# Attention block on one core: the next image's statistics and normalisation placed one by one on ScalarE, and the last residual loads given tiles and a queue of their own

## The chip, the cores and the metric

The kernel runs on one core of one Trainium2 chip. A core has five engines that run beside each other and meet at semaphores: TensorE (matmul, PE in the profile; its weight loads are PEld), VectorE (DVE), ScalarE (ACT), GpSimd (POOL) and SyncE (SP). SP, ACT and POOL each also have a queue on which DMA transfers are issued. The metric is device microseconds of one execution; the kernel before takes 3188.57 us, the median of 5 runs (3187.05 to 3190.02).

## The reference, cut to what matters

The input x has 16 images of 512 channels and 32 x 32 = 1024 pixels, in float32. Each image is normalised in 8 groups of channels, goes through attention with 4 heads of 128 channels over its 1024 pixels, is projected, and is added to itself.

```
mu, var = mean and variance of each group of channels
xn  = (xg - mu) * rsqrt(var + EPS) * gamma + beta
q, k, v = split(einsum('oc,bchw->bohw', qkv_w, xn) + qkv_b, 3)
attn = softmax(einsum('bhnd,bhmd->bhnm', q, k) * dh ** -0.5)
out = einsum('bhnm,bhmd->bhnd', attn, v)
out = einsum('oc,bchw->bohw', proj_w, out) + proj_b
return x + out
```

The last line is the residual: x has to be read a second time where the projection's results are ready.

## The kernel before, in words

The whole work is one stream of steps (`steps` = 16 images x 4 heads x 8 key blocks). In step s the main loop does two halves. In each half it gives TensorE the scores of one key block against 512 queries (`scores`, matmul L789, into one of two PSUM banks s) and the weighted sum of the step before (`weighted_sum`, L885, into po). ScalarE turns the scores into exponentials p (L795) and VectorE adds p to the running denominator tot (L803). Behind the two matmuls of a half stands half of the step's *units*: pieces of other work that `plan_head` (L1027) writes by hand into a list `plan[j]` for each of the head's 8 key blocks j. The first half of the list runs in the first half of the step, the rest in the second.

Head 0 of an image carries the q and k projection of its own heads 2 and 3, head 1 the output projection of the image *before* (`proj_groups`, names pp), head 2 the q and k projection of the *next* image's heads 0 and 1, and head 3 the next image's v. So what the next image needs must be ready by the end of head 1: its x is loaded there (`load_x`, in `plan[0]`), its statistics are taken, and it is normalised in place. In image 0 head 1 has no output projection, and in the last image no next image.

The statistics are `stats_chunk` for each of 4 chunks of 128 channels (two passes over 128 x 1024 on ScalarE, L243 and L246, with small scalings L244, L245 and L249 between them) and then `stats_group` once, which calls `Norm.group`: mean (L50, VectorE), a small matmul pm (L52, TensorE), d, mu and d2 (L55 to L61) and vv (L59) on VectorE, a small matmul pv (L63), ve (L65, VectorE), rstd as a power on GpSimd (L67), and sc, t and sh on VectorE (L69, L76, L78). `normalise` is one ScalarE instruction over 128 x 512 (L85, x<-x,sh,sc); there are 8 for an image, 4 chunks by 2 halves. `x_sums` (L280) then forms sums of the normalised x on VectorE. Before, `plan_head` puts two `stats_chunk` at the end of each of `plan[2]` and `plan[3]`, `stats_group` at the end of `plan[4]`, and four `normalise` at the end of each of `plan[5]` and `plan[6]`.

The projections are a matrix product in two levels of seven products instead of eight. The outer level has four groups g (`OUTER`); in each group, the inner level (`strassen`, L445) runs the products p1, p2, p6, p5, p7, p4, p3 in two PSUM banks x and y (matmuls L564). Between them ScalarE copies bank x out (p1, u2, u3: L458, shown as pp_u, pp_p) and bank y is added to such a copy by VectorE (L584) into a result tile r. The next product into a bank waits until the copy has been made. The inner results are c11, c22, c21 and c12; `combine` (L631) joins the groups' results, and `finish` (L766) adds bias and residual: for each 128 x 512 piece of an image's output one VectorE instruction y = r + bias + y (L769), one y = y + r (L772), and a DMA to out (L773).

The residual y is loaded by `prepare` (L753), two pieces for each of c11, c22, c21 and c12: into a tile of `ypool`, which has 4 buffers, by GpSimd's queue (L756). A fifth load therefore waits until an earlier piece has been stored. The c12 pieces, loaded for the last group, are the last two of the eight. `tpool` has one buffer for each tag; its tags ot40 and ot41 hold sums of the heads' outputs (t4) that TensorE reads in the output projection. SP's queue carries the weights of the groups (L371).

Which engine runs what is fixed in the code; the order on each engine is made by a scheduler that follows the program's order, except that `tc.high_priority(URGENT)` lets exponentials and the copies between products go ahead of other work. `tc.issue_after(ins)` keeps the instructions within it from being placed ahead of `ins`. [...]

```
for half in range(NH2):
    scores(s, half)
    weighted_sum(s - 1, half)
    n = (len(units) + 1) // 2
    run(units[half * n : (half + 1) * n])
```

Of the kernel before, what the change touches and what calls it, by code (L numbers as in the profile page):

```python
# [10 lines left out]
F32 = mybir.dt.float32  # L11
# [5 lines left out]
P = 128  # L17
# [4 lines left out]
HALF = 512  # L22
# [133 lines left out]
KC = 2  # L156
# [6 lines left out]
def fast_path(ctx, tc, x, sources, out, consts, flag, dims):  # L163
# [6 lines left out]
    nc = tc.nc  # L170
    B, C, N, NCC, NH2, NB, GC, SCALE = dims
# [9 lines left out]
    tpool = ctx.enter_context(tc.tile_pool(name="t", bufs=1))  # L181
# [7 lines left out]
    ypool = ctx.enter_context(tc.tile_pool(name="y", bufs=4))  # L189
# [44 lines left out]
    def stats_chunk(b, c):  # L234
        if c == 0:
            mvs[b] = gn.tile([P, NCC, 2], F32, tag="mv", name=f"mv_{b}")
        if b == 0:
            norm.chunk(mvs[b], xs[b, c], c)
            return

        junk = lpool.tile([P, N], F32, tag="tt", name=f"junk_{b}_{c}")
        sums = gn.tile([P, 3], F32, tag="st", name=f"sums_{b}_{c}")
        nc.scalar.activation(junk, xs[b, c], AF.Identity, accum_out=sums[:, 0:1])  # L243
        nc.scalar.mul(mvs[b][:, c, 0:1], sums[:, 0:1], 1.0 / N)  # L244
        nc.scalar.mul(sums[:, 1:2], sums[:, 0:1], -1.0 / N)  # L245
        nc.scalar.activation(  # L246
            junk, xs[b, c], AF.Square, bias=sums[:, 1:2], accum_out=sums[:, 2:3]
        )
        nc.scalar.mul(mvs[b][:, c, 1:2], sums[:, 2:3], 1.0 / N)  # L249

    def stats_group(b):
        mu, sc = norm.group(mvs.pop(b))
        scaled[b] = sc, norm.shift(mu, sc)

    def normalise(b, c, half):
        t = xs[b, c][:, ts(half, HALF)]
        sc, sh = scaled[b]

        return norm.apply(t, t, sc, sh, c, b > 0 or c % 2 == 1)
# [16 lines left out]
    def sums_of_b(b, rows=(1, 2, 3), chunks=range(KC)):  # L276

        def sub(o, i, j):
            for k in chunks:
                nc.vector.tensor_sub(b[o][k], b[i][k], b[j][k])  # L280

        if 1 in rows:
            sub("t1", "b12", "b11")
        if 2 in rows:
            sub("t2", "b22", "t1")
        if 3 in rows:
            sub("t3", "t2", "b11")
            sub("t4", "b21", "t2")

    def x_sums(b, rows=(1, 2, 3)):  # L290
        if 1 in rows:
            xb[b] = halves([xs[b, c] for c in range(NCC)], "x")
        sums_of_b(xb[b], rows)

    def o_blocks(b):
        ob[b] = halves([os_[b, h] for h in range(HEADS)], "o")
# [35 lines left out]
    def stage_blocks(site):  # L332

        raw = raw_blocks(site)
        st = stage[site] = {}
        names = ("a11", "a12", "a21", "a22", "s1", "s2")
        if site in ("proj", "v"):
            for n in names[:4]:
                st[n] = ypool.tile([P, HALF], F32, tag="y", name=f"st_{n}")
            for i, n in enumerate(names[4:]):  # L340
                st[n] = tpool.tile([P, HALF], F32, tag=f"ot2{i}", name=f"st_{n}")
        else:
            for i in range(3):
                t = opool.tile([P, N], F32, tag="o", name=f"st_{site}_{i}")
                for h in range(2):
                    st[names[2 * i + h]] = t[:, ts(h, HALF)]
        for n in names[:4]:
            load_block(st[n].rearrange("p (s d) -> p s d", d=P), raw[n])
# [397 lines left out]
    def proj_groups(b):  # L746

        ys = {}

        def place(which, r):  # L750
            return 2 * (int(which[1]) - 1) + r, int(which[2]) - 1

        def prepare(which, r):  # L753
            o, half = place(which, r)
            t = ys[which, r] = ypool.tile([P, HALF], F32, tag="y", name=f"y_{b}_{o}_{half}")
            dma = nc.gpsimd.dma_start(t, x[b, ts(o, P), ts(half, HALF)])  # L756

            tc.add_manual_dep(
                dma.ins, last_eviction[b].ins.name,
                mybir.DependencyInfo(  # L760
                    mybir.DependencyClass.Sync, mybir.DependencyReason.DATA
                ),
                reason="residual",
            )

        def finish(which, r, a, c):  # L766
            o, half = place(which, r)
            t = ys.pop((which, r))
            nc.vector.scalar_tensor_tensor(  # L769
                t, a, projb_sb[:, o : o + 1], t, ALU.add, ALU.add  # L770
            )
            nc.vector.tensor_add(t, t, c)  # L772
            nc.gpsimd.dma_start(out[b, ts(o, P), ts(half, HALF)], t)  # L773

        return two_levels(f"pp_{b}", "proj", b, lambda: ob[b], finish, prepare=prepare)
# [3 lines left out]
    inverse, rows_of, added, exps = {}, {}, {}, {}  # L779
    steps = B * HEADS * NB  # L780

    def where(s):
        bh, j = divmod(s, NB)
        return (*divmod(bh, HEADS), j)
# [112 lines left out]
    def spread(plan, units, first, last):  # L897

        for i, u in enumerate(units):
            plan[first + i * (last - first) // len(units)].append(u)  # L900
# [15 lines left out]
    def kept_group(site, g):  # L916
        if g == 0:
            stage_sums(site)
        group_weights(site, g, True)

    def staggered(lists):


        starts = (0, 4, 8, 16)[: len(lists)] if len(lists) != 3 else (0, 4, 10)
        at = [(a + i, g, u) for g, (a, us) in enumerate(zip(starts, lists))
              for i, u in enumerate(us)]
        return [u for _, _, u in sorted(at, key=lambda t: t[:2])]
# [33 lines left out]
    def last_projection(b):  # L961
# [12 lines left out]
        def add(row, r, half, a, done):  # L974
            o = 2 * row + r
            t = y[o][:, ts(half, HALF)]
            nc.vector.tensor_add(t, t, a)
            if done:
                (nc.sync, nc.scalar)[r].dma_start(out[b, ts(o, P), ts(half, HALF)], t)
# [43 lines left out]
        for r in range(2):  # L1023
            mm(y_[r], r, 3, False)
            add(0, r, 1, y_[r], True)

    def plan_head(b, h):  # L1027

        plan = [[] for _ in range(NB)]
        if h == 0:  # L1030
            spread(plan, staggered(next_qk.pop()), 0, NB)
            if b > 0:
                plan[6].append(lambda: o_blocks(b - 1))
                plan[6].append(lambda: sums_of_b(ob[b - 1]))
            else:
                plan[5].append(lambda: stage_blocks("v"))
        elif h == 1:
            if b > 0:
                spread(plan, staggered(proj_groups(b - 1)), 0, NB)
            if b + 1 == B:  # L1040
                plan[0].append(lambda: last_loads("x"))
            else:
                plan[0].append(lambda: load_x(b + 1))
                spread(plan, [lambda c=c: stats_chunk(b + 1, c) for c in range(NCC)], 2, 4)
                plan[4].append(lambda: stats_group(b + 1))
                for r in range(2):
                    plan[5 + r] += [
                        lambda c=c, half=half: normalise(b + 1, c, half)
                        for c in range(KC * r, KC * r + KC) for half in range(NH2)
                    ]  # L1050
                plan[6].append(lambda: x_sums(b + 1, (1,)))
            if b == 0:
                for g in range(len(OUTER)):
                    plan[g // 2].append(lambda g=g: kept_group("v", g))
                    plan[NB // 2 + g].append(lambda g=g: kept_group("proj", g))
                plan[2].append(lambda: stage_blocks("proj"))
                spread(plan, [lambda o=o: bias_of_v(o) for o in range(NCC)], 3, 5)
        elif b + 1 == B:
            if h == 2:
                plan[0].append(lambda: last_loads("w"))  # L1060
                plan[2].append(last_bias)
            else:
                os_[b, h] = opool.tile([P, N], F32, tag="o", name=f"o_{b}_{h}")
                plan[3].append(lambda: o_blocks(b))
                plan[3].append(lambda: sums_of_b(ob[b], (1,)))
                plan[5].append(lambda: sums_of_b(ob[b], (2, 3), (0,)))
        elif h == 2:
            spread(plan, staggered(qk_groups(b + 1, 0)), 0, NB)

            plan[0].insert(2, lambda: x_sums(b + 1, (2,)))  # L1070
            plan[1].append(lambda: x_sums(b + 1, (3,)))
        else:

            spread(plan, staggered(next_v.pop()), 0, NB - 1)

            plan[NB - 2].append(lambda: ahead[f"qk_{b + 1}_1"]())
        return plan
# [33 lines left out]
    plan = []  # L1111
    for s in range(steps + 1):
        units = []
        if s < steps:
            b, h, j = where(s)
            if j == 0:
                plan = plan_head(b, h)
# [157 lines left out]
```

## Time and profile before

| what | value |
|---|---|
| median of 5 runs | 3188.57 us (3187.05 to 3190.02) |
| profiled execution, its own time | 3187.58 us |
| its span in the profile | 3185.8 us |
| TensorE busy | 3156.0 us (99%), granted clock 1.00 |
| VectorE busy | 2632.2 us (83%) |
| ScalarE busy | 1443.6 us (45%) |
| GpSimd busy | 527.7 us (17%) |
| one image in the middle | 196.4 us |
| L85, normalisation, each (124 in all, 4 of them image 0's own) | 810 ns |
| L756, residual loads | 120, of 256 KB each |

An image in the middle repeats every 196.4 us, so head 1 of image 6 lies at about 1276 to 1325 us. In the lines below, a timeline shows start (us), duration (us), engine, line of the code, operation, out<-in with shapes, a count of equal instructions that were merged into one row, and in brackets how long the engine stood still before it and who ended that. A float32 matmul shows as two records; each runs on into the next, so TensorE's pace is read from start to start and not from the durations.

### The profile page before, as it was taken

What the parts mean: (1) busy time and instruction counts of PE and PEld (TensorE: products, weight loads), DVE (VectorE), ACT (ScalarE), POOL (GpSimd) and SP (SyncE); (2) the same over time, 40 slices, a digit from 0 to 9 for tenths busy, and PEclk for the clock granted to TensorE, in tenths of its full rate; (3) what the DMA queues carried; (4) which work ended last, traced back from release to release, by engine and by line L of the source; (5) the groups of instructions that cost most, each with busy time, mean ns of one, the idle gap of its engine ahead of it and who ended that gap; (6) DMA issues with size and microseconds to landing.
All of it is one profiled execution on the core that took longest, in us unless ns stands there. A gap on an engine that the chain in (4) does not pass through costs nothing.

```text
span 3185.8 us, 34047 instructions
## 1 busy us (share of the span) xinstructions
PE 3156.0 (99%) x10474; PEld 2182.5 (69%) x10474; DVE 2632.2 (83%) x4625; ACT 1443.6 (45%) x2709; POOL 527.7 (17%) x922
## 2 busy tenths in 40 slices
PE   8999999999999999999999999999999999999999
PEld 6566676676766766667666767667666676766764
DVE  8878878788897888878888787987879878788784
ACT  2535435354353543535435354453534545344342
POOL 0011221111211112211122111222112221122200
PEclk9999999999999999999999999999999999999999
DMA  5654554545545455454554545555355553555531
GB/s 169 216 184 153 188 174 151 172 147 196 169 159 167 153 184 174 164 167 143 194 170 161 175 137 189 172 171 177 132 178 169 175 179 133 184 160 183 182 126 41
DMA packets 209387, 526.92 MB, mean 165 GB/s; under 512 B 32816, under 2 KB 65840, under 8 KB 209200
## 3 DMA queue, kind: packets, MB, share of 16 engines
q1 hardware_dynamic: 128992, 276.88, 27.6%
q0 software_dynamic: 66240, 212.39, 19.6%
q10 hardware_dynamic: 13968, 35.41, 3.5%
q8 instruction: 86, 1.41, 0.2%
q14 instruction: 101, 0.83, 0.1%
HBM read 389.56 MB, written 135.00 MB: 165 GB/s over the span
## 4 chain that ended last, share of the span: by engine, by line
PE 85%; issue 5%; DVE 4%; DMA 2%; ACT 2%; POOL 1%; SPq 0%; ACTq 0%; POOLq 0%; DVEq 0%
PE po L885 24%; PE s L789 23%; PE qk_x L564 12%; PE qk_y L564 9%; PE v_x L564 6%; PE v_y L564 4%; PE pp_x L564 4%; PE pp_y L564 3%; ACT x L85 1%; DVE pp_r L631 1%; DMA y<-in_x 1%; POOL rstd L67 1%; DMA out_y<-y 1%; DVE pp_r L584 1%; DVE tot L803 1%
## 5 line engine op out<-in xcount | busy, mean ns | idle before, releaser
L885 PE MATMUL po<-p,v 128*128 128x512 f32 x2048 | 1048.9, 594 | 0.0
L789 PE MATMUL s<-qk,qk 128*128 128x512 f32 x2048 | 1047.1, 593 | 1.3 <-ACT p L795 1.3
L795 ACT ACTIVATE p<-s 128x512 f32<-128x512 f32 x1024 | 610.8, 597 | 944.6 <-PE s L789 904.2
L885 PEld LDWEIGHTS po<-p,v 128*128 128x128 f32 x2048 | 602.9, 303 | 316.8 <-issue 212.1
L803 DVE TENSOR_TENSOR tot<-tot,p 128x1024 f32<-128x1024 f32 x385 | 470.1, 1221 | 162.4 <-ACT p L795 162.4
L789 PEld LDWEIGHTS s<-qk,qk 128*128 128x128 f32 x2048 | 387.6, 190 | 89.2 <-issue 28.0
L564 PEld LDWEIGHTS qk_x<-qk_t,w 128*128 128x128 f32 x1344 | 250.6, 190 | 171.3 <-issue 76.4
L564 PE MATMUL qk_x<-qk_t,w 128*128 128x256 f32 x1344 | 357.2, 382 | 1.1 <-ACT qk_u L458 1.1
L458 ACT COPY qk_u<-qk_x 128x512 f32<-128x512 f32 (+1 forms) x256 | 136.4, 533 | 232.2 <-PE qk_x L564 224.5
L728 POOL DMA_DIRECT2D vd<-vu x120 | 66.6, 557 | 909.5 <-DVE vu L720 905.9
L584 DVE TENSOR_TENSOR qk_r<-qk_y,qk_u 128x512 f32<-128x512 f32 (+1 forms) x256 | 158.7, 620 | 36.3 <-ACT qk_u L458 22.2
L564 PE MATMUL pp_x<-pp_t,w_proj 128*128 128x256 f32 x630 | 169.4, 385 | 6.1 <-ACT pp_u L458 5.8
L773 POOL DMA_DIRECT2D out_y<-y x120 | 66.2, 552 | 615.2 <-DVE y L772 585.2
L733 POOL DMA_DIRECT2D v<-vd x240 | 140.5, 592 | 162.7 <-DMA vd<-vu 64.9
L584 DVE TENSOR_TENSOR v_r<-v_y,v_u 128x512 f32<-128x512 f32 (+1 forms) x120 | 76.1, 634 | 110.6 <-ACT v_u L458 80.3
L564 PE MATMUL v_x<-v_t,w_v 128*128 128x256 f32 x630 | 166.6, 381 | 0.0
L538 POOL DMA_DIRECT2D kept_t<-qk_t x240 | 129.2, 540 | 224.1 <-DVE qk_t L534 158.2
L564 PEld LDWEIGHTS pp_x<-pp_t,w_proj 128*128 128x128 f32 x630 | 115.4, 190 | 73.3 <-issue 22.2
L564 PEld LDWEIGHTS v_x<-v_t,w_v 128*128 128x128 f32 x630 | 118.4, 190 | 55.3 <-issue 19.1
L564 PE MATMUL qk_y<-x,w 128*128 128x256 f32 x512 | 141.7, 379 | 0.0
L663 DVE SCALAR_TENSOR_TENSOR qk<-qk_r,qkb_sb,qk_r 128x512 f32<-128x512 f32 x192 | 137.9, 746 | 1.6
L458 ACT COPY v_u<-v_x 128x512 f32<-128x512 f32 (+1 forms) x124 | 66.3, 535 | 160.2 <-PE v_x L564 130.3
(204 smaller groups left out, 4489.1 us busy)
## 6 DMA issues: line engine op xcount, KB each, us to landing
kept_t<-qk_t POOLq DMA_DIRECT2D x180, 256.0 KB, 3.1
w<-kept SPq DMA_DIRECT2D x90, 512.0 KB, 4.1
v_t<-kept_t SPq DMA_DIRECT2D x180, 256.0 KB, 2.9
w<-kept SPq DMA_DIRECT2D x90, 384.0 KB, 3.4
rinv<-row ACTq DMA_DIRECT2D x63, 512.0 KB, 4.8
x<-in_x POOLq DMA_DIRECT2D x60, 512.0 KB, 5.0
vd<-vu POOLq DMA_DIRECT2D x120, 256.0 KB, 3.0
v<-vd POOLq DMA_DIRECT2D x240, 128.0 KB, 4.0
```

Of the source, the lines that this page charges most:

```text
L458: nc.scalar.copy(t[n][:, :width], t["x"][:, :width])
L538: nc.gpsimd.dma_start(t, to)
L564: nc.tensor.matmul(acc[:, ts(i, Q)], have["w"][t][:, i, slot, :], inner(i, bn), start=(first and i == 0), stop=True, skip_group_check=True,)
L584: nc.vector.tensor_add(dst, view(a), view(c))
L663: nc.vector.scalar_tensor_tensor(st[b, h][:, ts(half, HALF)], a, qkb_sb[:, i : i + 1], c, ALU.add, ALU.add)
L728: nc.gpsimd.dma_start(rows[which][ts(h, P), :], u)
L733: nc.gpsimd.dma_start(vs[b, pair][ts(q, BLK), half].rearrange("m h (k i) j -> m (h k) (i j)", k=n), rows[which].rearrange("(k m) (q e) -> ...
L773: nc.gpsimd.dma_start(out[b, ts(o, P), ts(half, HALF)], t)
L789: nc.tensor.matmul(sc, ks[b, h][:, ts(j, P)], qs[b, h][:, ts(half, HALF)], start=True, stop=True)
L795: exps[s] = nc.scalar.activation(ps[s][:, ts(half, HALF)], sc, AF.Exp, scale=SCALE)
L803: added[b, h, j] = nc.vector.tensor_add(tot[b, h][:, i], tot[b, h][:, i], ps[s][:, i])
L885: nc.tensor.matmul(po[b, h][:, i], v_block(b, h, j), ps[s][:, i], start=(j == 0), stop=(j == NB - 1),)
```

## The change

In `prepare`, the c12 pieces take tiles of `tpool` with tags ot40 and ot41 in place of `ypool`'s, and are loaded by SP's queue in place of GpSimd's. In `plan_head`, the units of the next image's statistics and normalisation are laid one by one into successive half key blocks by a new helper `single`: the four `stats_chunk` from the second half of key block 1 to the first half of block 3, `stats_group` at the end of block 3, seven `normalise` from the second half of block 4 to the second half of block 7, and the eighth at the end of block 7. Another new helper, `behind_exps`, keeps each `stats_chunk` and `normalise` behind the latest exponential issued so far. No computation is added or left out.

```
         def prepare(which, r):
             o, half = place(which, r)
-            t = ys[which, r] = ypool.tile([P, HALF], F32, tag="y", name=f"y_{b}_{o}_{half}")
-            dma = nc.gpsimd.dma_start(t, x[b, ts(o, P), ts(half, HALF)])
+            own = which == "c12"
+            t = ys[which, r] = (tpool if own else ypool).tile(
+                [P, HALF], F32, tag=f"ot4{r}" if own else "y", name=f"y_{b}_{o}_{half}"
+            )
+            eng = nc.sync if own else nc.gpsimd
+            dma = eng.dma_start(t, x[b, ts(o, P), ts(half, HALF)])
...
+    def behind_exps(f, *args):
+        with tc.issue_after(exps[max(exps)].ins):
+            f(*args)
+
+    def single(plan, first, works):
+        for i, f in enumerate(works):
+            j, half = divmod(2 * first + 1 + i, 2)
+            plan[j].insert(len(plan[j]) if half else (len(plan[j]) + 1) // 2, f)
...
                 plan[0].append(lambda: load_x(b + 1))
-                spread(plan, [lambda c=c: stats_chunk(b + 1, c) for c in range(NCC)], 2, 4)
-                plan[4].append(lambda: stats_group(b + 1))
-                for r in range(2):
-                    plan[5 + r] += [
-                        lambda c=c, half=half: normalise(b + 1, c, half)
-                        for c in range(KC * r, KC * r + KC) for half in range(NH2)
-                    ]
+                single(plan, 1, [
+                    lambda c=c: behind_exps(stats_chunk, b + 1, c) for c in range(NCC)
+                ])
+                plan[3].append(lambda: stats_group(b + 1))
+                single(plan, 4, [
+                    lambda c=c, half=half: behind_exps(normalise, b + 1, c, half)
+                    for c in range(NCC) for half in range(NH2)
+                ][:7])
+                plan[NB - 1].append(lambda: behind_exps(normalise, b + 1, NCC - 1, 1))
                 plan[6].append(lambda: x_sums(b + 1, (1,)))
```

## The prediction

> **What bounds the kernel now.** I read the page first: busy shares, then the chain that ended last.
>
> ```profile
> PE 3156.0 (99%) x10474; PEld 2182.5 (69%) x10474; DVE 2632.2 (83%) x4625; ACT 1443.6 (45%) x2709; POOL 527.7 (17%) x922
> PE 85%; issue 5%; DVE 4%; DMA 2%; ACT 2%; POOL 1%; SPq 0%; ACTq 0%; POOLq 0%; DVEq 0%
> ```
>
> TensorE is busy all the time, at a granted clock of 1.0, and the change touches no matmul. So the only thing to win is time in which TensorE waits. Busy shares cannot show that, because neighbouring matmul records overlap. I therefore went through TensorE's timeline: while nothing is late, a 512-column matmul starts 0.86 us after the one before it, a 256-column one 0.43 us. Summed over the span, the starts lie 40.6 us further apart than that. Most of it is at the two ends, in image 0, or in the tiny matmuls. Two waits repeat where head 1 of an image ends and head 2 begins, among the work that the change moves. The timelines of 1313 to 1332 us (image 6) show both, TensorE first:
>
> ```profile
> 1320.66 1.02 PE L789 MATMUL s<-qk,qk 128*128 128x512 f32 x2
> 1322.10 0.70 PE L564 MATMUL pp_x<-pp_t,w_proj 128*128 128x256 f32 x2 [0.41 <-ACT pp_u L458]
> ...
> 1329.10 0.59 PE L564 MATMUL qk_y<-qk_t,w 128*128 128x256 f32 x2
> 1330.44 0.70 PE L564 MATMUL qk_y<-qk_t,w 128*128 128x256 f32 x2 [0.74 <-DVE qk_t L534]
> ```
>
> From 1320.66 the next start should be 1321.52; it is 1322.10, 0.58 late. From 1329.10 it should be 1329.53; it is 1330.44, 0.91 late. The pair that follows a wait also takes 0.70 instead of 0.59, about 0.1 more.
>
> ScalarE shows the first cause:
>
> ```profile
> 1318.60 0.59 ACT L795 ACTIVATE p<-s 128x512 f32<-128x512 f32 x1
> 1319.09 1.51 ACT L85 ACTIVATE x<-x,sh,sc 128x512 f32<-128x512 f32 x2
> 1320.50 0.58 ACT L795 ACTIVATE p<-s 128x512 f32<-128x512 f32 x1
> 1320.98 0.81 ACT L85 ACTIVATE x<-x,sh,sc 128x512 f32<-128x512 f32 x1
> 1321.68 0.36 ACT L458 COPY pp_u<-pp_x 128x256 f32<-128x256 f32 x1
> ```
>
> Eight normalisations (L85, 0.71 from start to start) came as one lump from 1315.25. The copy that frees bank pp_x stood behind them until 1321.68, though its matmul ended at 1320.82.
>
> The second cause is on VectorE and on GpSimd's queue:
>
> ```profile
> 1326.45 0.76 DVE L769 SCALAR_TENSOR_TENSOR y<-pp_r,projb_sb,y 128x512 f32<-128x512 f32 x1
> 1328.09 0.75 DVE L769 SCALAR_TENSOR_TENSOR y<-pp_r,projb_sb,y 128x512 f32<-128x512 f32 x1 [0.88 <-DMA y<-in_x]
> 1328.76 1.29 DVE L772 TENSOR_TENSOR y<-y,pp_r 128x512 f32<-128x512 f32 x2
> 1329.96 0.42 DVE L534 TENSOR_TENSOR qk_t<-x 128x256 f32<-128x256 f32 x1
> ```
>
> ```profile
> 1322.59 0.54 POOL L756 DMA_DIRECT2D y<-in_x  x1 [0.60 <-DMA out_y<-y]
> 1323.76 0.54 POOL L756 DMA_DIRECT2D y<-in_x  x1 [0.63 <-DMA out_y<-y]
> ```
>
> The last two residuals (c12) take tiles that earlier outputs still hold. Their loads are issued at 1322.59 and 1323.76, the second lands 4.3 us later, and VectorE stands still with qk_t queued behind it.
>
> **The change part by part.**
>
> 1. *The lump goes.* The ScalarE wait of the kind above stands in the timeline 15 times in images 1 to 14 (0.43 to 0.61 us; image 3 has it twice): 8.5 us. The slow pair behind each: 15 x 0.1 = 1.5. Gone: 10.0 us.
>
> 2. *The c12 residuals get tiles ot40 and ot41 and SP's queue.* The VectorE wait reached TensorE in 6 of 14 images: 0.29, 0.32, 0.91, 2.18, 0.61, 0.36, together 4.7 us, and 0.5 for the slow pairs. Gone: 5.2 us. In the new order (the order in which the changed program's instructions stand on each engine and queue) the two loads wait only for TensorE's last readers of ot40 and ot41, in projection group 2. That is some 13 and 12 us before VectorE wants them, laid out with the rows' durations, and the nearest rows for landing are 3.9 (y on GpSimd's queue, median) and 2.9 to 5.5 us (256 KB weights on SP's queue). Behind them on SP stand weight loads (L371) that wait for about the same matmuls, so they lose an issue, 0.33 us by L938's row, out of a lead of over 8 us. Cost nothing; without that cover each microsecond late would cost 14. GpSimd loses 30 issues of 0.54 us, off the path.
>
> [...]
>
> 3. *Statistics later, group earlier.* No instruction is added or dropped on ScalarE: 8 x 0.71 and 4 x about 2.5 us per image, as before, in another order. The first chunk moves from behind the second o eviction to two exponentials later, and the last chunk ends about one key block later. The group's small matmuls pm and pv move one block earlier. They now stand on TensorE just behind their inputs: mean follows the VectorE addition at L772, and pm follows mean. In the row sums pm comes out 0.1 late. Three more near misses are the inner c22 evictions of groups 2 and 3 (0.03 each) and a qk_t (0.1). Bounds: nothing, or all four with a slow pair each, 0.25 + 4 x 0.1 = 0.65 per image. I take 0.35 (one slow pair), for 14 images 4.9 us.
>
> 4. *The new wait: the first L85 stands ahead of the copy of pp_2's bank x.* L85 waits for sh; behind it on ScalarE are that copy, which TensorE needs, and an exponential. I sum both sides from the end of pp_1's last y matmul, with start-to-start times of the rows. VectorE and on: 0.2 to see it, eviction 0.60, vv 0.08, L772 0.60, L631 1.13, ve 0.15; 0.15 to GpSimd, rstd 1.88, back 0.04; sc 0.08, o 1.13, t 0.08, L631 1.13, sh 0.15; L85 0.04 + 0.71, copy 0.59, and 0.05 to TensorE: 8.8 us. TensorE meanwhile has eight 256-column matmuls (3.46), six of 512 (5.16) and pv (0.31): 8.9 us. A tie, 0.1 to spare. It rests on GpSimd being free at ve. Ahead of rstd now stands a y load that waits for the first out_y. Before, from that out_y to that y load it took 1301.86 to 1304.43, 2.6 us, and so in 13 of 14 images (3.2 in the other); laid out in the new order, up to 3.1 us stay hidden, because a second out_y is issued in between. Bounds: nothing, or 0.5 us (0.03 of slip in each of the eighteen links) and a slow pair in each image, 8.4 us. I take 0.1 per image, 1.4 us, because the rows of these links repeat to some 0.02 us.
>
> [...]
>
> 5. *Image 0.* There TensorE lost 1.6 us (1.7 with the pairs) to exponentials behind L85, at 142 and 146 us, but at 155.75 it waits for weights whose load hangs on VectorE and DMA. What it gains there it waits for here. Bounds 0 and 1.7 gained; I take 0.
>
> Sum: -10.0 - 5.2 + 4.9 + 1.4 = -8.9 us. The profiled execution took 3187.58 us (span 3185.8 and 1.8 around it), 1.0 below the median of 3188.57. So 3178.7 for that execution and 3179.7 for the median. I say **3179.5**.
>
> **Rivals.** About 0.2%, 6.4 us, is what a measurement of this kernel can tell from no change.
>
> *Faster by under 0.2%: the wait moves.* The tie of part 4 is lost by half a microsecond in every image, since its eighteen links may each slip. For: the spare time is 0.1 us. Against: the rows repeat. 14 x (0.5 + 0.1) = 8.4 in place of 1.4: 3179.5 + 7 = 3186.5. That the change does not spread the work as it says belongs here: the new order still has L85 in twos between exponentials late in the head.
>
> *Slower: rstd caught behind the y load on GpSimd.* Place: the first y load ahead of L67, which waits for out_y. For: the second such wait took 3.1 to 5.8 us from issue to issue, so such landings occur. Against: the first took 2.6 nearly always. Past 3.2 us (3.1 and the spare 0.1) each microsecond costs TensorE one per image. The sign turns where 14 images eat 8.9 us, 0.64 more than I take for each, at about 3.9; 0.2% slower is passed at 1.1 more, about 4.3. At 4.8: 1.6 + 0.1 per image, 24 in place of 1.4, so 3179.5 + 22.4 = 3202.
>
> *All waits go and none comes:* -15.2 and 1.7 in image 0: 3171.7.
>
> **How the numbers follow.** My sum 0.55, of which a fifth comes out just short of 0.2%; the wait moves 0.27; caught on GpSimd 0.13; all goes 0.05. Faster by over 0.2% (below 3182.2): 0.55 x 0.8 + 0.05 + a few of the second case, 0.52. Within: 0.35. Slower: 0.13. Range 3172 to 3193: it takes in the clean end and the first microseconds of the slow case. The own range of my sum, by the bounds of parts 3 and 4: 3173 to 3192.
>
> **What would show it.** Right: no wait for pp_u at an s of inner group 3; no DMA y<-in_x among VectorE's waits; y at SP; L85 in ones and twos. Part 4: TensorE's start after the po ahead of pp_2's last x matmuls, and the time from ve to rstd. Wrong: a wait of over 0.3 us there or at pm in each image, SP weights landing late, or qk_y still waiting for qk_t.

## The result, and the profile after

The changed kernel takes **3184.01 us** (median of 23 runs, 3182.23 to 3193.47), the kernel before 3190.27 us beside it (43 runs, 3187.05 to 3194.66). The ratio is 0.9982, 95% interval 0.9977 to 0.9988: 6.3 us faster, just short of the 0.2% that the prediction set as its bound, and 4.5 us above the 3179.5 that it named. The profiled execution took 3185.32 us (span 3183.5). That of before, 3187.58, is 2.7 us below the median which 43 runs now show, and that of the changed kernel lies 1.3 above its median, so the two traces differ by 2.3 us only. What follows counts within the traces; the other 4 us of the 6.3 lie between executions, and nothing here shows what made them.

The page of the changed kernel, busy time and chain:

```profile
PE 3159.2 (99%) x10474; PEld 2184.0 (69%) x10474; DVE 2627.4 (83%) x4625; ACT 1447.0 (45%) x2709; POOL 511.0 (16%) x892
PE 91%; issue 4%; ACT 2%; DVE 1%; DMA 0%; POOL 0%; SPq 0%; POOLq 0%; DVEq 0%
```

DMA (2% before) and VectorE (4%) have all but left the chain. Both waits that the prediction showed are gone: no pp_x waits for a copy behind s, no qk_y for qk_t. The sum of TensorE's late starts, counted as in the prediction, fell only from 40.6 to 38.4 us. By stretch:

| late starts of TensorE, us | before | after |
|---|---|---|
| up to image 0's head 1 | 5.9 | 6.2 |
| image 0's head 1 (118 to 165 us) | 5.9 | 8.5 |
| images 1 to 14 (165 to 3080 us) | 26.2 | 21.1 |
| tail | 2.6 | 2.5 |

Two new losses took most of the gain. The first stands in each of images 1 to 14. TensorE in image 6, and VectorE at the same time:

```profile
1303.62 0.59 PE L564 MATMUL pp_y<-o,w_proj 128*128 128x256 f32 x2
1304.38 0.36 PE L52 MATMUL pm<-mean,avg 128*128 128x4 f32 x2 [0.16 <-DVE mean L50]
1304.60 0.68 PE L564 MATMUL pp_y<-ot,w_proj 128*128 128x256 f32 x2
```

```profile
1303.47 0.69 DVE L778 TENSOR_TENSOR y<-y,pp_r 128x512 f32<-128x512 f32 x1
1304.07 0.16 DVE L50 COPY mean<-mv 128x4 f32<-128x4 f32 x1
```

From 1303.62 pm should start at 1304.05 (a 256-column matmul is two records, 0.43); it starts at 1304.38, because mean stands behind a residual addition that VectorE began 0.3 us before ScalarE had the fourth chunk's sum ready (L244 ended at 1303.81). The wait is 0.33 us in all 14 images (4.6), and pm's own second record is late as well (1.05 in all).

The second loss is image 0's. There pm waits 2.1 us for mean at 131 us, and later TensorE runs at half its rate for a while (granted clock 0.50 from 143 to 145 us). The window from 140 to 146 us of the changed kernel (length, then busy us and instructions of PE, PEld, DVE, ACT and POOL, the granted clock, DMA share, GB/s):

```profile
140.00:146.00 6.00, 6.00 (x22) 3.44 (x22) 4.49 (x13) 2.82 (x5) 0.00 (x0) 0.72 0.53 175
```

The clock reads 0.72; in the kernel before it reads 1.00 there:

```profile
140.00:146.00 6.00, 5.44 (x13) 2.20 (x12) 6.00 (x14) 5.97 (x10) 0.00 (x0) 1.00 0.77 258
```

Four matmul records in a row start 0.34 to 0.42 us late, 1.6 us in all. Three kernels of the experiments keep this image 0 as it is. With the statistics part alone the slow spell is there again (0.72 from 140 to 146 us); with own tiles on GpSimd's queue and with SP's queue and shared tiles pm waits 1.9 and 2.1 us too, but no spell follows (late starts in image 0 of 6.6 and 6.9 us, against 8.3 and 8.5 with the spell). So 1.6 of the 2.6 us that image 0 lost is this spell, which does not come every time.

The place that part 4 worried about, ScalarE at the first L85 and TensorE behind it:

```profile
1312.62 0.81 ACT L85 ACTIVATE x<-x,sh,sc 128x512 f32<-128x512 f32 x1 [1.31 <-DVE sh L78]
1313.34 0.57 ACT L458 COPY pp_u<-pp_x 128x512 f32<-128x512 f32 x1
```

```profile
1313.09 1.02 PE L891 MATMUL po<-p,v 128*128 128x512 f32 x2
1313.96 1.13 PE L564 MATMUL pp_x<-pp_t,w_proj 128*128 128x256 f32 x4
```

L85 waits 1.31 us and the copy behind it is done just as po is: pp_x starts 0.87 after it, on time. Over the 14 images this place cost 0.9 us, in two of them. These are small cases of the prediction's slower rival, rstd caught behind the y load on GpSimd; at 1902 us, where 0.63 was lost:

```profile
1898.01 0.54 POOL L762 DMA_DIRECT2D y<-in_x  x1 [1.43 <-DMA out_y<-y]
1898.57 1.03 POOL L67 TENSOR_TENSOR rstd<-ve,neghalf 128x4 f32<-128x4 f32 x1
```

The y load waits for an output issued 4.6 us earlier (3.1 in image 6, 4.2 in the other image), and rstd stands behind it.

One more row changed that the prediction had not looked at, VectorE's waits (in all, times, longest). First before, then after:

```profile
DVE sc L69 <- POOL rstd L67: 14.5, 15, 1.5
...
DVE y L769 <- DMA y<-in_x: 5.0, 7, 2.2
```

```profile
DVE sc L69 <- POOL rstd L67: 7.4, 16, 1.0
```

The wait for y is gone, and the idle time of VectorE ahead of sc is halved. That belongs to the group's new place, where an eviction of 0.69 us fills part of the time in which GpSimd computes rstd: with the residual part alone it is 14.0 us, with the statistics part alone 7.4.

### The profile page after: what moved, and what is told of

It reads as the page before. It is cut to its first block, busy times and chain, and to the rows that moved or that the text cites. A ratio compares the mean times of both kernels' runs of the same rounds, so it can differ in the third digit from the quotient of the medians.

```text
span 3183.5 us, 34109 instructions
## 1 busy us (share of the span) xinstructions
PE 3159.2 (99%) x10474; PEld 2184.0 (69%) x10474; DVE 2627.4 (83%) x4625; ACT 1447.0 (45%) x2709; POOL 511.0 (16%) x892
## 4 chain that ended last, share of the span: by engine, by line
PE 91%; issue 4%; ACT 2%; DVE 1%; DMA 0%; POOL 0%; SPq 0%; POOLq 0%; DVEq 0%
PE s L795 25%; PE po L891 25%; PE qk_x L564 12%; PE qk_y L564 9%; PE v_x L564 6%; PE v_y L564 4%; PE pp_x L564 4%; PE pp_y L564 4%; ACT junk L246 0%; ACT p L801 0%; PE v_x L681 0%; PE lx L975 0%; ACT junk L243 0%; PE v_y L681 0%; DVE pp_t L534 0%
## 5 line engine op out<-in xcount | busy, mean ns | idle before, releaser
L584 DVE TENSOR_TENSOR qk_r<-qk_y,qk_u 128x512 f32<-128x512 f32 (+1 forms) x256 | 158.8, 620 | 35.9 <-ACT qk_u L458 21.7
```

What stands on the lines that cost most here:

```text
L584: nc.vector.tensor_add(dst, view(a), view(c))
```

## The experiments

"Late starts" are TensorE's in images 1 to 14 and in image 0's head 1, from each kernel's profile. Ratios are to the kernel before, run beside it.

| kernel | median, us | ratio, 95% interval | images 1 to 14 | image 0 |
|---|---|---|---|---|
| before | 3190.3 | | 26.2 | 5.9 |
| changed | 3184.0 | 0.9982 (0.9977 to 0.9988) | 21.1 | 8.5 |
| residual part alone | 3182.0 | 0.9973 (0.9963 to 0.9983) | 20.0 | 6.2 |
| statistics part alone | 3244.1 | 1.0165 (1.0151 to 1.0179) | 85.6 | 8.3 |
| before, po first | 3187.5 | 0.9989 (0.9980 to 0.9998) | 25.2 | 7.3 |
| own tiles, GpSimd's queue | 3185.2 | 0.9987 (0.9978 to 0.9996) | 21.7 | 6.6 |
| SP's queue, shared tiles | 3230.6 | 1.0124 (1.0109 to 1.0140) | 69.7 | 6.9 |
| rstd twice | 3203.0 | 1.0043 (1.0030 to 1.0056) | 36.0 | 8.4 |
| rstd three times | 3229.4 | 1.0120 (1.0104 to 1.0135) | 60.5 | 11.9 |
| four chunks earlier | 3184.1 | 0.9982 (0.9973 to 0.9991) | 20.2 | 8.3 |
| image 0 as before | 3182.9 | 0.9976 (0.9966 to 0.9986) | 20.5 | 6.7 |
| two chunks in one half | **3176.5** | **0.9957** (0.9943 to 0.9971) | 15.4 | 6.4 |
| and normalise later | 3177.0 | 0.9959 (0.9945 to 0.9973) | 14.6 | 6.2 |
| and image 0 in singles | 3178.4 | 0.9961 (0.9948 to 0.9975) | 14.3 | 7.3 |

### The two halves of the change, each alone

The residual part alone is the kernel before with the `prepare` of the changed one.

> The kernel before with one part of the change: the two c12 residuals get tiles ot40 and ot41 and SP's queue; statistics, group and normalisations stay where they were. My theory: the two parts add up. This one takes away the DMA y<-in_x among VectorE's waits and, with it, the waits of TensorE for qk_t (5.8 us with the slow pairs in the trace of before), and leaves all 15 ScalarE waits ahead of pp_x (8.5 us and the pairs); pm shows no new wait. Time 4 to 6 us below before (ratio about 0.9984). Rival: the residual loads were late only where ScalarE's lump had already shifted the order, so the two parts share one gain; then this kernel is within 1 us of before (0.9998 or more) and the qk_t waits stay or turn into others.

Measured: 3182.0 us, 8.2 below before where 4 to 6 was expected, and 2.0 below the whole change, though their intervals overlap. The waits for y are gone, as expected. The waits at pp_x behind the lump went too, which was not: of 8.5 us at pp_x, 1.9 are left, 0.14 in each image at an earlier pp_x. TensorE's timeline shows why:

```profile
1319.93 1.02 PE L795 MATMUL s<-qk,qk 128*128 128x512 f32 x2
1320.79 1.02 PE L891 MATMUL po<-p,v 128*128 128x512 f32 x2
1321.64 0.59 PE L564 MATMUL pp_x<-pp_t,w_proj 128*128 128x256 f32 x2
...
1327.68 0.59 PE L564 MATMUL qk_y<-qk_t,w 128*128 128x256 f32 x2
1328.43 0.70 PE L564 MATMUL qk_y<-qk_t,w 128*128 128x256 f32 x2 [0.15 <-DVE qk_t L534]
```

The scheduler now puts a po between s and the pp_x that used to wait; ScalarE's lump is the same. But each image has a new wait of 0.32 us at a qk_y, for VectorE's qk_t. So the 8.5 us were not simply gained: 14 x 0.32 = 4.5, the 1.9 left at pp_x, and slow pairs come back. The gain of this kernel, 6.3 us in images 1 to 14, is about what the y waits had cost (5.8 with their pairs).

The statistics part alone is the changed kernel with the old `prepare`.

> The changed kernel without its part on the residuals (c12 loads back in the shared y tiles and on GpSimd's queue). My theory: the 15 ScalarE waits go (-10.0 us), pm waits 0.33 us for mean in each of images 1 to 14 (4.6 us and some 3 us in the slow pairs behind it), image 0's first head loses about 2.6 us more than before, and the qk_t waits of some 5 us stay. Together within 2 us of before (ratio 0.9995 to 1.0005). Rival: the wait at pm is made by the residual part (VectorE's y add comes earlier or later with it); then pm shows no wait here and the time is 5 us or more below before (0.9985).

Measured: 3244.1 us, 54 us slower than before and far outside what both theories said. pm waits 0.33 us as expected, so that is the statistics' own; but in every image TensorE starts a qk_y 2.2 to 3.5 us late, because VectorE waits for residuals. VectorE, GpSimd and SP's queue in the image around 1350 us:

```profile
1353.24 1.42 DVE L769 SCALAR_TENSOR_TENSOR y<-pp_r,projb_sb,y 128x512 f32<-128x512 f32 x2 [3.44 <-DMA y<-in_x]
```

```profile
1343.10 1.14 POOL L773 DMA_DIRECT2D out_y<-y  x2 [10.61 <-DVE y L772]
...
1348.27 1.18 POOL L757 DMA_DIRECT2D y<-in_x  x2 [2.44 <-DMA out_y<-y]
```

```profile
1343.13 0.32 SPq L371 DMA_DIRECT2D w<-kept  x1
```

The y load waits for the output issued at 1343.10 to leave its tile, and 0.03 us behind that output SP issued a weight load. From that output to the y load it is 4.9 to 5.3 us in all 14 images here, with SP's load within 0.2 us of the output; in the kernel before, where SP's load stands 1.4 us ahead of the output, it is 3.1 to 3.3 us in 13 of 14. The fourteenth is the image that lost 2.18 us in the prediction, 5.0, though SP's load stood 1.4 us ahead there too. The kernel with SP's queue and shared tiles (below) adds a contrast within one trace: 4.8 to 5.2 us in the 13 images in which SP's load stands 0.02 or 0.03 us behind the output, and 2.8 in the one in which it stands 2.6 us ahead. So in these two traces the near coincidence goes with the late landing in every image, a late landing stands without it in one, and no run moved SP's load alone. The rest of the 54 us is for the most part a slower clock, told below: 0.993 granted over the span of 3247.8 us, against 1.000 before (by these, 0.007 x 3247.8, an estimate of 23 us).

### Own tiles or own queue

`eng = nc.gpsimd` for the c12 loads, tiles as in the change:

> The changed kernel, but the two c12 loads are issued on GpSimd's queue, still into their own tiles ot40 and ot41. My theory: the own tiles carry the whole gain of this part and the queue is worth nothing, so the time equals the changed kernel's within 1.5 us (ratio to before 0.9975 to 0.999) and VectorE waits for no residual. Rival: GpSimd's queue matters, because the loads stand there ahead of or behind rstd or an output, and the wait for them or for sh comes back; then 3 us or more slower than the changed kernel.

The time is the changed kernel's within the intervals, and VectorE waits for no residual. One image shows the prediction's slower rival at its largest: at 2094 us rstd stands behind a y load that waited for an output issued 5.1 us before, and pp_x starts 1.18 us late. The reverse, SP's queue with the shared tiles (`t = ys[which, r] = ypool.tile(..., tag="y")`):

> The changed kernel, but the c12 pieces take the shared y tiles again and are loaded by SP's queue. My theory: a load that needs a tile which an earlier output still holds waits for that output on whatever queue it stands, so the residuals are late again as in the run with the statistics part alone (2 to 3.5 us for qk_y in each image, 40 us and more in all), and SP's weight loads behind the waiting ones come late on top: 3225 us or more. Rival: the waits in that run came from GpSimd's queue, where the loads stood between outputs; then SP's queue cures most of it and the time is under 3200 us.

40 us slower than before; qk_y waits 1.6 to 2.7 us in each image, and VectorE waits for y as in the statistics part alone (1.91 us in the image at 1347 us). The tiles carry this part of the change, in the new order of the statistics at least; no run gave the old order own tiles on GpSimd's queue. With own tiles the second queue moved the time by less than the measurement can tell: 3184.0 us on SP's queue, 3185.2 on GpSimd's. With shared tiles it did move it: 3230.6 us on SP's queue, 3244.1 on GpSimd's. The waits at qk_y come to 28.4 us in the one trace and 37.0 in the other; why is not shown.

### Is a wait worth its length?

The prediction priced each wait at what it reads. This kernel takes away the wait at pp_x and nothing else, by putting po ahead of it in the kernel before:

```
                 plan[6].append(lambda: x_sums(b + 1, (1,)))
+                if b > 0:
+                    plan[NB - 1].insert(0, lambda: None)
```

> The kernel before with one edit: an empty unit at the head of the last key block's list pushes the last x product of projection group 3 half a key block on, so that on TensorE the po matmul of 0.86 us stands ahead of the pp_x that waits for ScalarE's lump. Nothing else changes: statistics, normalisation and residual loads as before. Theory of the prediction (each wait has its own price): the 15 waits of 0.57 us and their slow pairs go, as in the changed kernel, and the qk_t waits stay: 8 to 10 us below before (ratio 0.997). Theory formed since, from the run with the residual part alone: behind the lump stands VectorE, which has no idle time from rstd to head 2 and is late by nearly the same 0.45 us; the wait leaves pp_x and comes back in each image at pp_y or qk_y, and the time is within 2 us of before (ratio 0.9993 or more).

By the medians 3.0 us came of the 8 to 10 (the interval allows 0.6 to 6.4); late starts in images 1 to 14 fell by 1.0, from 26.2 to 25.2. 14 of the 15 waits at pp_x are gone, and in all 14 images the next product waits instead. TensorE, then VectorE:

```profile
1325.17 0.59 PE L564 MATMUL pp_x<-pp_t,w_proj 128*128 128x256 f32 x2
1326.12 0.70 PE L564 MATMUL pp_y<-o,w_proj 128*128 128x256 f32 x2 [0.36 <-DVE pp_r L584]
```

```profile
1324.52 1.22 DVE L803 TENSOR_TENSOR tot<-tot,p 128x1024 f32<-128x1024 f32 x1
1325.65 0.41 DVE L584 TENSOR_TENSOR pp_r<-pp_y,pp_u 128x256 f32<-128x256 f32 x1
```

pp_y is 0.52 late for an eviction that stands in VectorE's queue behind tot, and VectorE's rows follow each other without a break here. So behind ScalarE's lump stood VectorE, late by nearly as much. The second theory was right on the mechanism; its bound for the ratio (0.9993) was passed by 0.0004, within the interval.

### How exact is the tie?

The power computed twice and three times lengthens the chain to sh and leaves the result as it is:

```
         nc.gpsimd.tensor_tensor(rstd, ve, self.neghalf, ALU.pow)
+        nc.gpsimd.tensor_tensor(rstd, ve, self.neghalf, ALU.pow)
```

> The changed kernel with the power that gives rstd computed twice in a row on GpSimd, which makes the chain to sh 1.9 us longer. My theory (part 4): the first L85 waits for sh with pp_2's u3 copy behind it, and the two sides are within about 0.1 us of each other, so nearly all of the 1.9 us reaches TensorE in each of 14 images as a wait ahead of pp_x: 20 to 28 us slower than the changed kernel. Rival: there is more slack than the sum gives (the copy or L85 has other time to spare); then less than 10 us slower.

18.9 us over the changed kernel. GpSimd and TensorE:

```profile
1315.85 1.84 POOL L67 TENSOR_TENSOR rstd<-ve,neghalf 128x4 f32<-128x4 f32 x1
1317.77 1.01 POOL L68 TENSOR_TENSOR rstd<-ve,neghalf 128x4 f32<-128x4 f32 x1
```

```profile
1320.82 1.02 PE L892 MATMUL po<-p,v 128*128 128x512 f32 x2
1322.76 1.13 PE L565 MATMUL pp_x<-pp_t,w_proj 128*128 128x256 f32 x4 [0.92 <-ACT pp_u L459]
```

The second power takes 1.0 us and not 1.9, so the expected size was wrong (the first, too, takes 1.03 where it starts late, at 1898.57 above). pp_x is 1.07 to 1.29 late in each of 14 images (15.3 us). What was added arrived whole: there is no slack at this place.

> The changed kernel with the power computed three times. In the run with two, the second power took 1.0 us and TensorE waited 1.08 us for the copy behind L85 in each of 14 images, 15.3 us in all. Theory: there is no slack, so the third adds another 1.0 us per image, the wait becomes 2.0 to 2.1 us, 29 us over the changed kernel. Pauses of 1.9 us and more were followed in most cases by some 3.4 us at half the matmul rate, worth 1.4 to 1.8 us; if that follows from the pause, 8 or more of the 14 images show it here, the granted clock is below 0.998, and the time is 40 to 55 us over the changed kernel (3224 to 3240). Rival: those spells belong to the places where they were seen and not to the pause; then none appears and the time is 3213 us.

The wait is 2.16 or 2.17 us in 12 images and 2.24 and 2.41 in two, another 1.08 each, and the time 45 us over the changed kernel, at a clock of 0.996; 5 of the 14 images show the half rate, not 8.

### Moving the statistics

All four chunks half a key block earlier (`2 * first + late + i` in `single`, late = 0):

> The changed kernel with its four statistics chunks half a key block earlier; the group and the normalisations stay where the change put them. My theory: pm waits for mean because the last chunk, and with it the VectorE addition ahead of mean, ends too late; half a key block (some 1.7 us on VectorE) is more than the 0.33 us that it is late. The 14 waits at pm and the 2.1 us at pm in image 0 go, about 7 us of the 10 us that the new waits cost; if nothing else turns late the time is 6 to 8 us below the changed kernel (ratio to before about 0.996). Rival: the place is taken by evictions of the inner groups, which an earlier chunk puts behind VectorE's statistics work; each image then loses 0.3 to 0.7 us there and the time equals the changed kernel's within 2 us or exceeds it by up to 3.

The rival was right: pm's waits went, and in all 14 images pp_y waits 0.34 us for VectorE's eviction:

```profile
1324.58 0.70 PE L564 MATMUL pp_y<-o,w_proj 128*128 128x256 f32 x2 [0.18 <-DVE pp_r L584]
```

Image 0's pm still waits 1.9 us. The time equals the changed kernel's. Image 0 alone laid out as before (`if b == 0:` with the old lines):

> The changed kernel, but in image 0 statistics, group and normalisations of image 1 stand as in the kernel before; images 1 to 14 as changed. My theory: the 2.1 us wait at pm near 131 us goes, image 0's first head costs TensorE 5.9 us of late starts again and not 8.5, and the time is 2 to 3 us below the changed kernel (ratio to before about 0.9974). The granted clock, which fell to 0.72 between 140 and 146 us in the trace of the changed kernel, stays at 1.0 there if the drop follows the pause of 2 us. Rival: the drop has nothing to do with the pause; then it shows in this kernel too, or in no pattern, and the gain is at most 1 us.

Late starts in image 0 fall from 8.5 to 6.7 and the clock reads 1.00 from 140 to 146 us. The median is 1.1 us lower, less than expected and within the intervals. With that, chunks 2 and 3 in one half block, so that only the last two come earlier:

```
+    at(3, lambda: behind_exps(stats_chunk, b + 1, 0))
+    at(4, lambda: behind_exps(stats_chunk, b + 1, 1))
+    at(4, lambda: behind_exps(stats_chunk, b + 1, 2))
+    at(5, lambda: behind_exps(stats_chunk, b + 1, 3))
```

(`at(i, f)` puts f into half block i, by the same rule as `single`.)

> The changed kernel with image 0 as before, and with the second and third statistics chunk together in one half key block, so that only the third and the fourth come half a block earlier. My theory: pm waits because the fourth chunk's mean arrives while VectorE has already begun a residual addition of 0.6 us; a fourth chunk some 1 us earlier puts mean ahead of that addition, and what was wrong with moving all four was that the first two met other evictions. The 14 waits of 0.33 us at pm and the slow pairs behind them (about 7 us together) go and nothing comes in their place: 3175 to 3178 us, ratio to before about 0.9955, 5 to 7 us below the kernel that has only image 0 as before. Rival: VectorE has no room in this stretch, and whatever leaves pm shows up within the same image at an eviction (as the 0.34 us ahead of pp_y did when all four were moved); then 3182 to 3184 us.

3176.5 us, 13 below before and the best kernel of the study. VectorE and TensorE, to be read against the rows of the changed kernel above:

```profile
1299.39 0.16 DVE L50 COPY mean<-mv 128x4 f32<-128x4 f32 x1
1299.47 0.69 DVE L778 TENSOR_TENSOR y<-y,pp_r 128x512 f32<-128x512 f32 x1
```

```profile
1299.81 0.28 PE L52 MATMUL pm<-mean,avg 128*128 128x4 f32 x2
1299.95 0.68 PE L564 MATMUL pp_y<-o,w_proj 128*128 128x256 f32 x2
```

mean now passes ahead of the addition, and pm starts 0.86 after the po of 1298.95, on time. Late starts in images 1 to 14 fall by 5.1 against the kernel with image 0 as before, where pm's waits and its late second record had cost 5.7; only one wait is new, 1.0 us for a qk_y at 1826 us. VectorE's idle time at sc is 5.7 us.

Two further steps brought nothing that can be told apart. The first normalisation a key block later:

> As the run with two chunks in one half, and the first normalisation one key block later, so that it stands behind the u3 copy and no longer ahead of it; the eight then follow in ones to threes. My theory: the tie of part 4 (the first L85 waiting for sh with the copy behind it) cost under 1 us in all, so its removal gains at most 1 us over that run; the rarer waits from po to pp_x (0.2 to 0.6 us in one to three images) disappear. Rival: later normalisations end too late for head 2's first matmuls or lump again ahead of a copy; then 3 us or more slower than that run, with waits for pp_p, pp_u or x.

And image 0's normalisations one by one:

> The best kernel so far (two chunks in one half key block, image 0 as before) with the normalisations of image 0 also laid one by one behind exponentials. Theory: image 0's two waits of exponentials behind L85 (0.72 and 0.86 us, with the pairs 1.8 us) go, and the time is 1 to 2 us below that kernel. Rival: what is gained there is waited for at 156 us, where the first qk_x hangs on weights; then within 1 us.

In the latter, image 0's exponentials wait less (0.92 in place of 0.72 and 0.86), and a qk_x then waits 1.71 us at 162 us for ScalarE's copy qk_u: the rival's kind of outcome, at another instruction than it named.

## Why the prediction was right, and where its steps were not

The direction held, and the time lies in the range; but the range of 3172 to 3193 is 21 us wide and holds the time of before too, so that says little. The sum did not come out where the traces can be counted: it has 8.9 us fewer late starts in images 1 to 14 and nothing in image 0, and they show 5.1 fewer there and 2.6 more in image 0. Part 1 priced a gain that was hardly there, and parts 3 and 5 priced the new losses too low. That the medians fell by 6.3 us, nearer to the forecast than the traces, is not explained by these steps; as far as they go it is luck.

1. *The lump goes* (-10.0). The waits went, all 15. Read as a gain of its own the step **failed**: the kernel with po first took nearly all of the same waits away, and late starts fell by 1.0 and the median by 3.0, because VectorE was late by nearly the same amount. The statistics part on top of the residual part changed images 1 to 14 from 20.0 to 21.1.
2. *Own tiles and queue* (-5.2). Right in mechanism and nearly in size: the qk_y waits of 5.8 us are gone, VectorE waits for no load, and the residual part alone gains 6.3 in images 1 to 14. That the tiles carry it is shown in the new order (3185.2 us with own tiles on GpSimd's queue, 3230.6 with shared tiles on SP's). What the step missed is that the new statistics order needs these tiles: without them it costs 54 us.
3. *Statistics later, group earlier* (+4.9). This term was **mis-sized**. The near misses at the c22 evictions and at qk_t stayed misses; pm alone cost 4.6 in waits and 1.05 in its own second record, and the place of pm and pv ahead of 256-column pairs instead of s another 1.8 (the slow pairs at pm, pv and pp that the best kernel keeps, 9.2 against 7.4 before). Together 7.4, and some 9 on the prediction's own terms, since the 7.4 of slow pairs before hold the 1.5 that part 1 takes off. The row sum had pm 0.1 late; it was 0.33, of which 0.18 is mean's end and 0.15 the step from mean to pm (part 4 takes 0.05 for such a step).
4. *The new wait at the first L85* (+1.4). Right: 0.9. The tie is as tight as stated, since each added 1.08 us of the chain reached TensorE as 1.08 us. The tie counts only if the copy stays behind the waiting L85, and there it stayed: in all 14 images of the changed kernel it starts 0.72 us after that L85 (1313.34 after 1312.62), and with rstd twice, where L85 waits 2.39 us in place of 1.31, again 0.72 (1322.14 after 1321.42).
5. *Image 0* (0). **Wrong**: it lost 2.6 us more than before, 1.6 of them in the slow spell that two other kernels with this image 0 do not show. The step looked only at what normalisation would gain; it did not ask what covers the wait from mean to pm in an image that has no projection work in head 1.

Of the rivals, the first, a wait that moves, describes best what happened, though the place was pm and not the L85; its time, 3186.5, lies nearer to 3184.0 than the forecast does. The slower rival occurred in two images of 14, at 4.2 and 4.6 us from output to y load, and cost 0.3 and 0.6 us there: less than the 1.0 and 1.4 that the prediction's rule gives, since rstd then took 1.0 us in place of 1.85 (the last section has the rows).

## What to carry to other kernels

A wait on the critical engine is worth its length only as far as the next engine behind it is early: before pricing it, ask when the next-latest input would have been ready (here ScalarE's copy was 0.57 us late and VectorE's eviction behind it 0.52). Try the parts of a change alone and together, because one part can be the cover without which the other costs 54 us. And look at what stands just ahead of a small instruction on which a matmul waits: moving two chunks by half a key block, so that mean (0.16 us) came ahead of an addition of 0.6, was worth as much as the whole change.

## What the runs showed of the hardware that was not expected

**Of 52 pauses of TensorE of 1.6 us or more, 30 were followed by a spell at half rate.** In the statistics part alone, around the pause of 2.9 us near 1353 us, the windows read:

```profile
1350.00:1356.00 6.00, 3.48 (x13) 2.20 (x11) 2.76 (x5) 1.99 (x4) 0.45 (x1) 1.00 0.50 164
1356.00:1360.00 4.00, 3.43 (x8) 2.17 (x9) 4.00 (x11) 0.59 (x1) 2.25 (x5) 0.65 0.72 265
1360.00:1366.00 6.00, 6.00 (x21) 4.17 (x20) 5.24 (x14) 2.37 (x4) 1.11 (x3) 0.95 0.54 175
```

Here the clock falls after the pause (0.65, then 0.95), not in it (1.00). Over the 14 traces, behind their first 100 us, 30 of the 52 late starts of 1.6 us or more were followed by a spell at a clock of 0.5. All but one of these spells last 3.4 us (the other 6.8); in them each record of a 512-column matmul starts 0.42 us late, which mostly costs 1.4 to 1.8 us. They began 0.3 to 2.0 us after the pause, but for three in image 0 that began 8.7 to 9.0 us after it, where the tie to the pause is weaker. (One more spell, at 150 us with rstd three times, began 11.7 us after a pause and is not counted.) All 7 pauses over 2.6 us had one, the shortest with one is 1.87, and at 2.16 to 2.18 it was 6 of 14. The four kernels without such a pause show none, nor do the 14 pauses of 1.08 us with rstd twice. So with its spell a pause of 2 us cost nearly twice what it reads (2 us and the 1.4 to 1.8); why some escape is not shown.

**The row of the power on GpSimd reads 1.01 to 1.05 us where nothing runs on VectorE at its start, and ends 0.9 us after tot where tot runs.** It reads 1.84 to 1.88 us in most images, 1.03 where it starts late, and a repeat right behind it 1.01. In the changed kernel, VectorE and GpSimd:

```profile
1307.85 1.22 DVE L809 TENSOR_TENSOR tot<-tot,p 128x1024 f32<-128x1024 f32 x1
```

```profile
1308.12 1.85 POOL L67 TENSOR_TENSOR rstd<-ve,neghalf 128x4 f32<-128x4 f32 x1
```

The power ends 0.90 us after tot does (1309.97 and 1309.07). Over the 14 traces all 157 rows of more than 1.5 us end 0.89 to 0.91 us after the VectorE instruction that was running when they started, which is tot in all but one; 65 rows with nothing running on VectorE took 1.01 to 1.05; and 13 that started while VectorE ran the eviction pp_r took 1.03 to 1.04; what sets tot and pp_r apart is not shown. So the 1.88 of the prediction was no price of the instruction alone, and while tot stands there a start up to some 0.8 us later would end no later, an estimate from the rows of 1.85 and 1.03. No run moved tot away from there, so that the power waits for VectorE is the author's reading of these ends.

**A store to HBM freed its tile 4.9 to 5.3 us after issue instead of 3.1 to 3.3** where a weight load was issued on SP within 0.2 us of it: the first in 14 images of the statistics part alone, the second in 13 of 14 of the kernel before (5.0 in the other, with no load within 0.2 us). That the one makes the other is argued from these, not shown by a run that moved only the load.
